# A 16-step gated recurrence in closed form: the scale of A moved into the gates, and 1 + d - t summed on TensorE

## The chip, the cores and the metric

The kernel runs on one core of a Trainium2 chip. The metric is the device time of one execution in microseconds, the median of three runs. The engines named below are TensorE (PE in the profile; its weight loads are PEld), VectorE (DVE), ScalarE (ACT), GpSimd (POOL) and SyncE (SP, which issues most of the transfers). Each engine works through its own queue of instructions in order; semaphores hold an instruction until the ones that it depends on, on other engines, are done.

## The reference

Four layers are applied one after the other to an image of 256 x 256 pixels and 128 channels in float32, each as x = x + layer(groupnorm(x)): an attention along rows, a gated complex recurrence, a triangle product and a convolution with a projection. The change concerns the second, cut here to what matters (c is 64, the channels are 64 real and 64 imaginary ones):

```python
forget_gate = jax.nn.sigmoid(x_ri @ Wf + bf + 2.0)
input_gate = jax.nn.sigmoid(x_ri @ Wi + bi)
delta = jax.nn.softplus(x_ri @ Wd + bd) * 0.1
A_f = _pad_and_fft(A_real, A_imag, h, w, k)
B_f = _pad_and_fft(B_real, B_imag, h, w, k)
...
mag = jnp.sqrt(Ar ** 2 + Ai ** 2 + 1e-08)
scale = 0.95 * jax.nn.sigmoid(mag) / (mag + 1e-08)
Ar = Ar * scale
Ai = Ai * scale
...
inp_r = delta[..., :c] * input_gate[..., :c] * Bx_r
inp_i = delta[..., c:] * input_gate[..., c:] * Bx_i
fg_r, fg_i = (forget_gate[..., :c], forget_gate[..., c:])
def step(h_state, _):
    h_r, h_i = h_state
    Ah_r = Ar * h_r - Ai * h_i
    Ah_i = Ar * h_i + Ai * h_r
    return ((fg_r * Ah_r + inp_r, fg_i * Ah_i + inp_i), None)
h0 = (jnp.zeros_like(x_r), jnp.zeros_like(x_i))
(h_r, h_i), _ = jax.lax.scan(step, h0, None, length=T)      # T = 16
```

For every pixel and channel, a step multiplies the pair (h_r, h_i) by a 2 x 2 matrix M and adds the same input v. M has the trace t = (fg_r + fg_i) Ar and the determinant d = fg_r fg_i (Ar^2 + Ai^2). The kernel doesn't run the 16 steps: it gets their sum from t, d, powers of M by repeated squaring, and a division by D = 1 + d - t.

## The kernel before

The recurrence (function `recurrence`) works on 64 blocks of 4 image rows. A block is held as tiles of 128 partitions (two halves of the block times 64 channels) by 2 x 512 elements (real and imaginary part, 512 pixels each), called wide in the code, or by 512 elements, called thin. All is float32.

A block passes through some seventy steps, each a small function of one or a few instructions of one engine. They are put in order by hand, in the list `order` at the end of the function: each entry is a step and a lag. Iteration `it` runs the list once, each step on block `it` minus its lag, so three blocks are in work at a time. `pin` keeps every engine's instructions in that order. Each engine's queue is therefore the list, filtered for that engine.

For TensorE one iteration is, with the block's lag in brackets: av (2), m2 (0), zb (1), pox, po1, po2 (2), zf (0), zi (1), bx (1), zd (0), za (0), pa (1), and av again. In the profile m2 is shown as m, and the three parts of po as po<-xf, po<-t and po<-yf. zd, zf and zi are the gates' products of weights and x. za and zb are the spectra of A and B. m2 and pa are sums of two squares, by an identity matrix (`ident`) as the weights and accumulation in PSUM; bx and av are complex products, summed in the same way with `ident` and its negative (`negid`). A float32 matmul shows as two passes.

For VectorE the end of an iteration and the beginning of the next are: s, u4, A, tr8, qg, u8, v (reads bx), xa, y1, y0, tr16, ff, xb, d_, pf, be, t, e_, yf (reads av), al, D_, t1, yb, tr2, p0, p1 (they read zb), u2, q, tr4. In the profile xa, xb and be show as g, y0 and y1 as y, t1, e_ and al as t, yb as yf, and p0 and p1 as p.

The steps around the change: za gives the unscaled A; zaa (ScalarE) copies it to `ar`; a2 and m2 give its squared magnitude; lm, mg, lb, iv, sg (ScalarE) and s (VectorE) give the scale s. A multiplies `ar` by s. A2 (ScalarE) squares the result, pa sums the two squares, d_ multiplies pa by ff = fg_r fg_i. pf gives fg_r + fg_i, t multiplies it by the real part of A, D_ makes 1 + d - t, and lD and eD (ScalarE: Ln and Exp) make the division. y0 and y1 multiply v by A, yf multiplies the result by f.

PSUM places are shared by tags: the gates and spectra rotate through two places ("z"), av, bx and po share a single one ("y"), m2 and pa rotate through two ("s"). A tile that takes a place waits until the readers of its predecessor are done. On ScalarE, Ln and Exp on the one hand and the sigmoids on the other need different tables, and the order keeps each group together, with two table loads for an iteration.

Of the kernel before, what the change touches and what calls it, by code (L numbers as in the profile page):

```python
# [10 lines left out]
AF = mybir.ActivationFunctionType  # L11
# [6 lines left out]
P = 128  # L18
N = 256
# [11 lines left out]
class Kernel:  # L31
# [808 lines left out]
    def recurrence(self, x1T, x2T, HD_, stats1, shift1, stats2, shift2):  # L840
# [5 lines left out]
        MUL, ADD, SUB, MAX = ALU.mult, ALU.add, ALU.subtract, ALU.max  # L846
        NB = N // 4
        with ExitStack() as c:
# [3 lines left out]
            negid = wp.tile([P, P], F32, name="negid")  # L852
            V.tensor_scalar_mul(negid, self.ident, -1.0)
            gw, gb = {}, {}
            with self.pool(name="rwp", bufs=2, space=PSUM) as ps0:
                ab, mg, _ = self.group_affine(wp, ps0, stats1, self.g4, "1", True, shift=shift1)
# [22 lines left out]
            D = [{} for _ in range(NB)]  # L879
            rows = lambda t: t.rearrange("p i (r v) -> p r i v", v=N)  # L880
            both = lambda t: t.unsqueeze(1).to_broadcast([P, 2, 512])
# [4 lines left out]
            def act(out, in_, func, **kw):  # L886
                want = tables.get(func)
                if want not in (None, current[0]):
                    pin(nc.scalar.preload_act_table_set(want))  # L889
                    current[0] = want  # L890
                return pin(self.act(out, in_, func, **kw))
# [13 lines left out]
            def wide(d, n, bufs=1):  # L905
                d[n] = tp.tile([P, 2, 512], F32, name=n, tag="w" + n, bufs=bufs)
                return d[n]

            def thin(d, n, bufs=1):
                d[n] = tp.tile([P, 512], F32, name=n, tag="h" + n, bufs=bufs)  # L910
                return d[n]

            def tt(out, a, b_, op):
                pin(V.tensor_tensor(out, a, b_, op))  # L914

            def stt(out, a, k, b_, op0, op1):
                pin(V.scalar_tensor_tensor(out, a, k, b_, op0, op1))  # L917
# [15 lines left out]
            def total(d, name, pairs):  # L933

                n = len(pairs)
                z = d[name] = ps.tile([P, n, 512], F32, name=name, tag="y" if n == 2 else "s", bufs=1 if n == 2 else 2)
                for i, terms in enumerate(pairs):
                    for k, (m, t) in enumerate(terms):
                        pin(self.mm(z[:, i], m, t, start=k == 0, stop=k == len(terms) - 1))

            def real_and_imaginary(d, name, p0, p1):

                total(d, name, [[(self.ident, p0[:, 0]), (negid, p1[:, 1])], [(self.ident, p0[:, 1]), (self.ident, p1[:, 0])]])

            def halves(d, out, name, z, func):
                for ri in range(2):
                    act(out[:, ri], d[z][:, ri], func, bias=gb[name][:, ri:ri + 1])
# [22 lines left out]
            def f(d): halves(d, wide(d, "f", 2), "f", "zf", AF.Sigmoid)  # L970
            def zi(d): gate(d, "i")
            def ig(d): halves(d, wide(d, "ig"), "i", "zi", AF.Sigmoid)
            def zaa(d): act(wide(d, "ar"), d["za"].rearrange("p r i v -> p i r v"), AF.Copy)
            def A(d):
                sb = d["s"].rearrange("p (r v) -> p r v", v=N).unsqueeze(2).to_broadcast([P, 2, 2, N])
                tt(rows(wide(d, "A", 2)), rows(d["ar"]), sb, MUL)
            def A2(d): act(wide(d, "A2"), d["A"], AF.Square)
            def pa(d): total(d, "pa", [[(self.ident, d["A2"][:, 0]), (self.ident, d["A2"][:, 1])]])
            def ff(d): tt(thin(d, "ff"), d["f"][:, 0], d["f"][:, 1], MUL)
            def pf(d): tt(thin(d, "fs"), d["f"][:, 0], d["f"][:, 1], ADD)  # L980
            def t(d): tt(thin(d, "t", 2), d["fs"], d["A"][:, 0], MUL)
            def d_(d): tt(thin(d, "d", 2), d["pa"][:, 0], d["ff"], MUL)
            def D_(d): stt(thin(d, "D", 2), d["d"], 1.0, d["t"], ADD, SUB)

            def xn(d):
                wide(d, "xn")
# [26 lines left out]
            def tr16(d): stt(thin(d, "tr16"), d["dn8"], -2.0, d["tq16"], MUL, ADD)  # L1013
            def xa(d): stt(thin(d, "g", 2), d["t"], -2.0, d["u8"], ADD, MUL)
            def xb(d): tt(d["g"], d["g"], d["tr16"], SUB)
            def lD(d): act(d["D"], d["D"], AF.Ln)
            def eD(d): act(d["D"], d["D"], AF.Exp, bias=math.log(0.5), scale=-1.0)
            def be(d): stt(d["g"], d["g"], 2.0, d["D"], ADD, MUL)
            def e_(d): stt(d["t"], d["t"], -1.0, d["g"], ADD, MUL)
            def al(d): tt(d["t"], d["u8"], d["t"], SUB)  # L1020

            def y0(d): tt(wide(d, "y0"), d["A"], both(d["v"][:, 0]), MUL)
            def y1(d): tt(wide(d, "y1"), d["A"], both(d["v"][:, 1]), MUL)
            def av(d): real_and_imaginary(d, "av", d["y0"], d["y1"])
            def yf(d): tt(wide(d, "yf"), d["av"], d["f"], MUL)
            def t1(d): tt(wide(d, "t1"), both(d["t"]), d["v"], MUL)
# [6 lines left out]
            def ordered(d, t, stop):  # L1033
                for half in range(2):
                    hs = slice(half * HC, (half + 1) * HC)
                    for ri in range(2):
                        pin(self.mm(d["po"][ri * HC:(ri + 1) * HC, half], self.ident[hs, hs], t[hs, ri], start=False, stop=stop))
# [7 lines left out]
            def bn(d):  # L1045
# [4 lines left out]


            order = (
                (zd, 0), (y0, 2), (tr16, 2), (za, 0), (xn, 1), (ff, 1), (A2, 1), (ab, 0), (pa, 1), (av, 2), (ae, 0),
                (xb, 2), (d_, 1), (eD, 2), (pf, 1), (a2, 0), (al_, 0), (be, 2), (zaa, 0), (dn2, 1), (t, 1), (dn4, 1),
                (m2, 0), (e_, 2), (lm, 0), (yf, 2), (zb, 1), (al, 2), (D_, 1), (t1, 2), (yb, 2), (pox, 2), (tq2, 1),
                (po1, 2), (po2, 2), (mg, 0), (tr2, 1), (lb, 0), (lD, 1), (zf, 0), (p0, 1), (p1, 1), (iv, 0), (u2, 1),
                (sg, 0), (tq4, 1), (ev_, 2), (f, 0), (q, 0), (tr4, 1), (s, 0), (dn8, 1), (zi, 1), (u4, 1), (A, 0),
                (bx, 1), (tq8, 1), (ig, 1), (tr8, 1), (qg, 1), (bn, 2), (u8, 1), (tq16, 1), (v, 1), (xa, 1), (y1, 1),
            )
            deep = max(lag for _, lag in order)  # L1060
# [525 lines left out]
```

## Time and profile before

| | |
|---|---|
| median of 3 runs | 5087.27 us (5086.96 to 5087.37) |
| span of the profiled execution, first to last instruction | 5083.0 us |
| its granted TensorE clock | 0.995 of full |
| attention and the first norm | up to about 1700 us |
| recurrence | about 1700 to 3219 us |
| triangle product and convolution | from about 3219 us |
| busy over the whole span | PE 4951.9, DVE 4100.4, ACT 3496.8, POOL 406.9 us |

The median stands 4.3 us above the span of the profiled execution. The shares over the whole span are averages over stages with different limits; the recurrence has to be read by itself. A matmul in the timeline is given its start and a modelled length; consecutive ones overlap, so the distance from start to start is the better measure of what one takes. "x4" in such a line is four passes, and the bracket at the end gives the idle time of the engine just before and what ended it.

### The profile page before, as it was taken

The numbers are of one execution on the slowest core, as the hardware profiler recorded it, in microseconds if no ns is written. First come the engines' busy times: TensorE is split into PE (matmuls) and PEld (weight loads), VectorE is DVE, ScalarE is ACT, GpSimd is POOL, SyncE is SP. The second block draws the span as 40 slices with busy tenths as digits, with TensorE's granted clock in tenths as the row PEclk, the third lists the DMA queues.
The fourth block names the chain that finished last, engine by engine and source line by source line (L and its number), as shares of the span: only waits on it lengthen the run. The fifth ranks groups of instructions, "written<-read, shape, count | busy, mean of one in ns | idle before, by whom it ended". The sixth has DMA issues, their size and how long they took to land.

```text
span 5083.0 us, 78992 instructions
## 1 busy us (share of the span) xinstructions
PE 4951.9 (97%) x31563; PEld 2715.8 (53%) x31563; DVE 4100.4 (81%) x4797; ACT 3496.8 (69%) x4948; POOL 406.9 (8%) x592
## 2 busy tenths in 40 slices
PE   8999999999999899999999999899999999999999
PEld 2444555555555333333333333329999953359999
DVE  6666999999999799999999999775333537779886
ACT  6445888888888899999999999453333357762110
POOL 0331000000000000000000000240111010000000
PEclk9999999999999999999999999999999999999999
DMA  8894222222222222222222221688667778865432
GB/s 290 292 338 173 88 80 84 84 80 88 84 80 84 68 68 68 72 64 76 64 73 67 72 68 60 218 324 309 237 229 243 252 286 321 324 233 180 142 122 67
DMA packets 204463, 781.69 MB, mean 154 GB/s; under 512 B 56278, under 2 KB 59628, under 8 KB 154788
## 3 DMA queue, kind: packets, MB, share of 16 engines
q1 hardware_dynamic: 146638, 505.57, 29.8%
q0 software_dynamic: 56160, 270.64, 14.8%
q8 instruction: 252, 4.13, 0.3%
q14 instruction: 117, 0.96, 0.1%
q10 hardware_dynamic: 1296, 0.40, 0.0%
HBM read 505.18 MB, written 271.32 MB: 153 GB/s over the span
## 4 chain that ended last, share of the span: by engine, by line
PE 57%; DVE 29%; issue 5%; ACT 1%; POOL 0%; DMA 0%; POOLq 0%; DVEq 0%; SPq 0%; ACTq 0%
PE z L60 9%; PE m L60 7%; PE nd L60 7%; PE sc L60 5%; PE zc L60 5%; PE po L60 4%; DVE tr L917 3%; DVE t L914 3%; DVE y L914 3%; DVE p L914 3%; DVE yf L914 3%; PE ppq L60 3%; PE ppv L60 2%; PE px L60 2%; PE pe L60 2%
## 5 line engine op out<-in xcount | busy, mean ns | idle before, releaser
L576 DVE TENSOR_TENSOR e<-sc,bT 128x1024 f32<-128x1024 f32 x512 | 603.1, 1220 | 49.8 <-PE sc L60 48.9
L54 ACT ACTIVATE e<-e 128x1024 f32<-128x1024 f32 x512 | 540.4, 1055 | 61.5 <-DVE e L576 52.4
L1077 DVE TENSOR_TENSOR LR<-z,sg 128x512 f32<-128x512 f32 x256 | 268.4, 1049 | 363.0 <-ACT sg L54 363.0
L60 PE MATMUL m<-U,v 128*128 128x128 f32 x4608 | 514.8, 275 | 0.0
L60 PEld LDWEIGHTS m<-U,v 128*128 128x128 f32 x4608 | 514.6, 192 | 0.0
L60 PE MATMUL z<-wf,zt 128*128 128x128 f32 x4096 | 459.6, 276 | 1.4 <-DVE zn L1077 1.4
L60 PEld LDWEIGHTS z<-wf,zt 128*128 128x128 f32 x4096 | 459.4, 192 | 2.3 <-DVE zn L1077 2.2
L54 ACT ACTIVATE sg<-z 128x512 f32<-128x512 f32 x256 | 152.9, 597 | 307.7 <-PE z L60 307.7
L54 ACT ACTIVATE sq<-zs 128x1024 f32<-128x1024 f32 x192 | 202.4, 1054 | 192.1 <-DVE zs L385 156.1
L576 DVE TENSOR_TENSOR ks<-e 128x1024 f32<-128x1024 f32 x256 | 301.0, 1217 | 0.0
L60 PE MATMUL sc<-tq,tk 32*128 32x256 f32 x4096 | 297.0, 401 | 3.0 <-DVE e L576 2.1
L60 PEld LDWEIGHTS sc<-tq,tk 32*128 32x128 f32 x4096 | 186.4, 184 | 159.6 <-issue 96.3
L60 PE MATMUL nd<-e,tv 128*32 128x256 f32 x4096 | 271.0, 382 | 0.0
L54 ACT ACTIVATE dn<-dn 128x512 f32<-128x512 f32 x384 | 241.9, 630 | 13.0 <-DVE dn L576 2.3
L60 PE MATMUL av<-y,ident 128*128 128x512 f32 x384 | 192.9, 611 | 44.0 <-DVE y L914 44.0
L60 PE MATMUL po<-LR 128*128 128x256 f32 x1024 | 222.2, 380 | 6.9 <-DVE LR L1077 6.9
L1462 ACT COPY m4s<-m 128x512 f32<-128x512 f32 x32 | 18.7, 583 | 287.2 <-PE m L60 287.2
L60 PEld LDWEIGHTS po<-LR 128*128 128x128 f32 x1024 | 194.1, 190 | 34.2 <-DVE LR L1077 7.7
L60 PE MATMUL bx<-p,ident 128*128 128x512 f32 x384 | 192.4, 610 | 0.0
L54 ACT ACTIVATE o<-po 128x256 f32<-128x256 f32 x256 | 84.3, 381 | 145.3 <-issue 110.5
L60 PEld LDWEIGHTS nd<-e,tv 128*32 128x32 f32 x4096 | 120.1, 109 | 108.2 <-issue 42.1
L889 ACT ACT_TABLE_LOAD x132 | 169.4, 1283 | 1.5
(366 smaller groups left out, 10321.1 us busy)
## 6 DMA issues: line engine op xcount, KB each, us to landing
zt<-znT SPq DMA_DIRECT2D x128, 1024.0 KB
znT<-zn POOLq DMA_DIRECT2D x64, 1024.0 KB, 5.2
xin<-x2T SPq DMA_DIRECT2D x64, 1024.0 KB
xin<-in_x_dram SPq DMA_DIRECT2D x50, 1024.0 KB
xr<-x3T SPq DMA_DIRECT2D x46, 768.0 KB
xT<-xo POOLq DMA_DIRECT2D x32, 1024.0 KB, 9.3
xr<-xT SPq DMA_DIRECT2D x64, 512.0 KB
zn<-znT SPq DMA_DIRECT2D x64, 512.0 KB
```

Of the source, the lines that this page charges most:

```text
L54: return self.nc.scalar.activation(out, in_, func, bias=bias, scale=scale, **kw)
L60: return self.nc.tensor.matmul(out, lhsT, rhs, start=start, stop=stop)
L576: pin = lambda f: lambda *a, **k: tc.keep_in_program_order(f(*a, **k))
L889: pin(nc.scalar.preload_act_table_set(want))
L914: pin(V.tensor_tensor(out, a, b_, op))
L917: pin(V.scalar_tensor_tensor(out, a, k, b_, op0, op1))
L1077: pin = lambda f: lambda *a, **k: tc.keep_in_program_order(f(*a, **k))
L1462: nc.scalar.copy(m4, m[4])
```

## The change

The scale s is no longer multiplied into A. It is multiplied into both forget gates instead, in place (`fs_`), which gives the same M, since every entry of M is a product of a gate and a part of A. A is then used unscaled as `ar` (now with two buffers, for it lives on until y0). The determinant is the product of the scaled gates times the unscaled squared magnitude, which m2 holds already; so the square A2 and its sum pa go. 1 + d - t is no longer made by VectorE: TensorE sums d and minus t in PSUM as pD (a tile of tag "s"), and lD reads that and adds the 1 as the bias of its Ln. In the list, D_ keeps its place, fs_ takes that of A, and A2 and pa leave.

```diff
-            def zaa(d): act(wide(d, "ar"), d["za"].rearrange("p r i v -> p i r v"), AF.Copy)
-            def A(d):
-                sb = d["s"].rearrange("p (r v) -> p r v", v=N).unsqueeze(2).to_broadcast([P, 2, 2, N])
-                tt(rows(wide(d, "A", 2)), rows(d["ar"]), sb, MUL)
-            def A2(d): act(wide(d, "A2"), d["A"], AF.Square)
-            def pa(d): total(d, "pa", [[(self.ident, d["A2"][:, 0]), (self.ident, d["A2"][:, 1])]])
+            def zaa(d): act(wide(d, "ar", 2), d["za"].rearrange("p r i v -> p i r v"), AF.Copy)
+            def fs_(d): tt(d["f"], d["f"], both(d["s"]), MUL)
             def ff(d): tt(thin(d, "ff"), d["f"][:, 0], d["f"][:, 1], MUL)
             def pf(d): tt(thin(d, "fs"), d["f"][:, 0], d["f"][:, 1], ADD)
-            def t(d): tt(thin(d, "t", 2), d["fs"], d["A"][:, 0], MUL)
-            def d_(d): tt(thin(d, "d", 2), d["pa"][:, 0], d["ff"], MUL)
-            def D_(d): stt(thin(d, "D", 2), d["d"], 1.0, d["t"], ADD, SUB)
+            def t(d): tt(thin(d, "t", 2), d["fs"], d["ar"][:, 0], MUL)
+            def d_(d): tt(thin(d, "d", 2), d["m2"][:, 0], d["ff"], MUL)
+            def D_(d): total(d, "pD", [[(self.ident, d["d"]), (negid, d["t"])]])
...
-            def lD(d): act(d["D"], d["D"], AF.Ln)
+            def lD(d): act(thin(d, "D", 2), d["pD"][:, 0], AF.Ln, bias=1.0)
...
-            def y0(d): tt(wide(d, "y0"), d["A"], both(d["v"][:, 0]), MUL)
-            def y1(d): tt(wide(d, "y1"), d["A"], both(d["v"][:, 1]), MUL)
+            def y0(d): tt(wide(d, "y0"), d["ar"], both(d["v"][:, 0]), MUL)
+            def y1(d): tt(wide(d, "y1"), d["ar"], both(d["v"][:, 1]), MUL)
...
-                (zd, 0), (y0, 2), (tr16, 2), (za, 0), (xn, 1), (ff, 1), (A2, 1), (ab, 0), (pa, 1), (av, 2), (ae, 0),
+                (zd, 0), (y0, 2), (tr16, 2), (za, 0), (xn, 1), (ff, 1), (ab, 0), (av, 2), (ae, 0),
...
-                (sg, 0), (tq4, 1), (ev_, 2), (f, 0), (q, 0), (tr4, 1), (s, 0), (dn8, 1), (zi, 1), (u4, 1), (A, 0),
+                (sg, 0), (tq4, 1), (ev_, 2), (f, 0), (q, 0), (tr4, 1), (s, 0), (dn8, 1), (zi, 1), (u4, 1), (fs_, 0),
```

The helper `total` makes pa, m2 and pD; it takes a PSUM tile of tag "s" for a single sum:

```python
z = d[name] = ps.tile([P, n, 512], F32, name=name, tag="y" if n == 2 else "s", bufs=1 if n == 2 else 2)
for i, terms in enumerate(pairs):
    for k, (m, t) in enumerate(terms):
        pin(self.mm(z[:, i], m, t, start=k == 0, stop=k == len(terms) - 1))
```

## The prediction

> **What bounds the kernel now.** I read the page first: TensorE (PE) is busy 97% of the span and VectorE (DVE) 81%, which does not say what limits the stage that the change touches. So next the busy time in stretches, for 600 us inside the recurrence:
>
> ```profile
> core 0: us, PE busy (x) PEld busy (x) DVE busy (x) ACT busy (x) POOL busy (x), PEclk, DMA share, GB/s
> 1900.00:2500.00 600.00, 583.98 (x1959) 194.21 (x1958) 600.00 (x749) 578.08 (x850) 13.88 (x26) 1.00 0.22 69
> ```
>
> VectorE has no gap at all: it is the bound. PE is short of it by 16 us in 600, ScalarE (ACT) by 22. But a PE busy time also counts matmuls stretched by waits, so the third view is the timeline of one steady iteration, PE first, then VectorE (start us, length us, engine, line, operation, tiles, idle before):
>
> ```profile
> 2204.48 1.10 PE L60 MATMUL av<-y,ident 128*128 128x512 f32 x2 [0.61 <-DVE y L914]
> ...
> 2207.99 1.88 PE L60 MATMUL m<-a,ident 128*128 128x512 f32 x4
> ...
> 2218.64 1.13 PE L60 MATMUL bx<-p,ident 128*128 128x512 f32 x2
> 2219.60 1.02 PE L60 MATMUL bx<-p,negid 128*128 128x512 f32 x2
> 2220.46 1.88 PE L60 MATMUL bx<-p,ident 128*128 128x512 f32 x4
> 2222.27 1.94 PE L60 MATMUL zd<-xf,gwd 128*64 128x512 f32 x8
> 2224.14 1.13 PE L60 MATMUL za<-ev,hs 14*128 14x512 f32 x4
> 2225.19 1.98 PE L60 MATMUL pa<-A,ident 128*128 128x512 f32 x4
> 2227.79 1.10 PE L60 MATMUL av<-y,ident 128*128 128x512 f32 x2 [0.61 <-DVE y L914]
> ...
> 2223.55 1.22 DVE L917 SCALAR_TENSOR_TENSOR v<-q,bx 128x1024 f32<-128x1024 f32 x1
> 2224.68 0.69 DVE L917 SCALAR_TENSOR_TENSOR g<-t,u 128x512 f32<-128x512 f32 x1
> 2225.28 2.36 DVE L914 TENSOR_TENSOR y<-A,v 128x1024 f32<-128x1024 f32 x2
> 2227.56 0.69 DVE L917 SCALAR_TENSOR_TENSOR tr<-dn,tq 128x512 f32<-128x512 f32 x1
> ```
>
> Two things are to be seen. The period is 23.30 us (av starts at 1738.75 in the first such iteration and 3160.06 in the last: 1421.31 / 61 = 23.30). And there is a loop round two engines: av on PE, then PE's queue down to bx, then v on VectorE (it reads bx), xa (shown as g), y1 and y0 (shown as y), and av of the next iteration. bx ends at 2220.46 + 1.88 = 2222.34, v starts at 2223.55: the loop has slack there, VectorE comes to v late because it is full. How long the loop is without that slack, the first full iteration shows, in which PE was late and VectorE waited:
>
> ```profile
> 1732.19 1.88 PE L60 MATMUL bx<-p,ident 128*128 128x512 f32 x4
> 1734.11 1.22 DVE L917 SCALAR_TENSOR_TENSOR v<-q,bx 128x1024 f32<-128x1024 f32 x1 [0.32 <-PE bx L60]
> 1738.75 1.02 PE L60 MATMUL av<-y,ident 128*128 128x512 f32 x2
> ...
> 1742.18 1.88 PE L60 MATMUL m<-a,ident 128*128 128x512 f32 x4
> 1743.99 1.13 PE L60 MATMUL zb<-ev,hs 14*128 14x512 f32 x4
> 1745.05 1.98 PE L60 MATMUL po<-xf,ident 128*128 128x512 f32 x4
> 1746.96 1.09 PE L60 MATMUL po<-t,ident 64*64 64x512 f32 x8
> 1747.87 1.04 PE L60 MATMUL po<-yf,ident 64*64 64x512 f32 x8
> 1748.84 1.94 PE L60 MATMUL zf<-xf,gwf 128*64 128x512 f32 x8
> 1750.64 1.94 PE L60 MATMUL zi<-xf,gwi 128*64 128x512 f32 x8
> 1752.51 1.12 PE L60 MATMUL bx<-p,ident 128*128 128x512 f32 x2
> ```
>
> v starts 0.04 us after bx ends (1732.19 + 1.88 = 1734.07), so a closed loop costs that. PE from av to bx took 1752.51 - 1738.75 = 13.76 us here, against 14.16 (2218.64 - 2204.48) in the steady state, where PE is held back a little at po and zi by VectorE. [...]
>
> [...] in both iterations above the matmuls come in the same order, and an early one never passes a late one. So the place of the new sum in PE's queue matters, not only its size. [...] the trace has 0.69, but successive ones start 0.60 apart, and 0.60 is what a removed one gives back. [...] Here pa is slow (3.25 us in place of 1.98) already behind a gap of 2.63 us at 3180.55, while 4 passes behind one of 1.32 us at 3213.86 took the usual 1.98; below I check the gap that arises.
>
> **The change, part by part**, for one iteration.
>
> VectorE: the product A (1024 wide) becomes f times s (1024 wide, one operand repeated over the two halves as in y0 and y1, 1.22 us): nothing either way. d_ reads m2 in place of pa, both in PSUM: nothing. D_ goes: -0.60 us. Its removal puts t1 directly behind al, whose result it reads; where an instruction follows its own source (fs then t, 1719.58 to 1720.30) starts are 0.72 apart, so +0.12. VectorE's work: 23.30 - 0.60 + 0.12 = 22.82 us. If that were all: 61 x -0.48 = -29 us.
>
> ScalarE: A2 goes, 0.95 us from start to start (2223.89 to 2224.83). lD reads PSUM: lm does that in 0.60 where lD takes 0.61 to 0.63; nothing. ScalarE is not the bound, so nothing is gained beyond room: lD now waits for the end of pD instead of D_. By the sums below pD ends 8.3 us after av, and lD starts in the steady iteration at 2212.11 - 2204.48 = 7.63, so iv, the table load, sg and the rest behind it move by about 0.7 us. f then ends at about 14.5 after av, and the product f times s comes up on VectorE at 15.0; qg, which needs ig, is ready near 16.8 against 16.7. Both stay 0.7 us short of where bx will let v go.
>
> TensorE: pa goes (4 passes, between za and av) and pD comes (4 passes, between zb and po). The total is equal, the place is not. pa stood behind bx, where PE waits for y0 in any case: its removal only lengthens the idle time before av. pD stands between av and bx, in the loop. Its price: bx is the same pattern as pD and po together, ident, negid, ident: 2222.27 - 2218.64 = 3.63 us. po alone takes 1746.96 - 1745.05 = 1.91. So pD adds 1.72 us. It doesn't wait itself: d and t are ready 2.3 and 4.1 us after av, pD starts at 6.4. Behind it in PE's queue stand po, zf, zi and bx; all move by 1.72 and bx takes v with it. Their own waits (yf, t1, yb, p1) are then long done. m2 is kept until d_ of the next iteration, at 1.6 to 2.3 us after av; the next m2 starts at 3.5 in the other place, and of the two PSUM buffers of that tag pa's goes to pD: nothing.
>
> The loop after the change: 13.76 (av to bx without holding) + 0.08 (av behind an idle PE, 2207.99 - 2204.48 = 3.51 against 3.43) - 0.03 (zf, held by p1 in that iteration; in the stage's first iteration zf takes 1706.97 to 1708.74 = 1.77) + 1.72 = 15.53 to the start of bx; + 3.70 to its end (2218.64 to 2222.34); + 0.04 to v; + 4.24 from v to av (2223.55 to 2227.79, VectorE's fixed order). Sum 23.51 us. Without pD it is 21.79, so the loop had 1.51 us of slack and the change puts 1.72 in it. VectorE at 22.82 is then no longer the bound and idles 0.7 us before v. PE's own work, 23.51 less 4.28 for the way from bx over v to av, plus zd and za beside it (1.87 + 1.05), is 22.15: it idles 1.4 us before av. That is about the gap of 1.32 us that did no harm, so I charge nothing for the clock.
>
> 61 periods x (23.51 - 23.30) = +12.8 us. Beginning and end: the first d no longer waits for A2 and pa (the trace has VectorE idle 4.8 us there, but most of it lies on other chains), worth -1 to -2; at the end pa leaves and pD comes in the chain: +1 to +2. Taken as 0, plus or minus 2. Span 5083.0 + 12.8 = 5095.8; the median of the runs stands 4.3 above the span, so 5100 us.
>
> Unknown costs, both ends: pD 1.60 (if ident behind zb comes as cheap as elsewhere) to 1.85 us; v after bx 0.0 to 0.1; av after the longer gap 0 to 0.1. A period of 23.35 to 23.75, +3 to +27 us: 5090 to 5114.
>
> **Rivals.** (a) The loop is shorter than I make it, VectorE stays the bound and the saved D_ counts: 22.82, 5087 - 29 = 5058 us. For it: VectorE at 600 of 600. Against: it needs pD to cost under 1.03 us on PE, or PE's 13.76 to hold 0.7 us of waiting that I took for work. The sign turns at a pD of 1.51 us. (b) Between the two: loop and old period agree within 0.1 us, 5081 to 5093, if more than I think of PE's time at po, zf and zi is waiting. (c) The moved ScalarE chain: if f and ig come over 1 us later than worked out, f times s holds VectorE's queue, and v waits for qg, not bx; a period of 24.1, +49, 5136 us. For it: ScalarE 578 of 600 busy. Against: A2's 0.95 us is gone. A clock that drops in the 1.4 us gap would be worse still.
>
> **How the numbers follow.** Main case 0.60, (a) 0.10, (b) 0.17, (c) with the clock 0.13. What can be told from no change is 0.2%, 10 us: 5077 to 5097. About three quarters of the main case lies above. Faster 0.11, same 0.28, slower 0.61. The range leaves out (a) and half of (c): 5083 to 5122; the main case's own is 5090 to 5114.
>
> **What would show it.** Right: v with an idle time before it released by PE bx in every iteration; av's idle at about 1.4 us; av to av 23.5; pD to po 1.8 us. Wrong: VectorE again full with a period under 23; or v's wait released by ScalarE.

## The result, and the profile after

| | before | changed |
|---|---|---|
| median | 5087.11 us | 5121.19 us |
| lowest to highest of 4 runs | 5086.85 to 5087.37 | 5118.82 to 5127.68 |
| ratio, 95% interval | 1 | 1.0069 (1.0055 to 1.0084) |
| span of the profiled execution | 5083.0 us | 5119.4 us |
| its mean TensorE clock | 0.995 | 0.99 |

The change makes the kernel slower by 0.7%, 34 us, where +13 was predicted. The stretch of the recurrence that was shown of before reads after the change (busy time of each engine, then granted clock, DMA share and GB/s):

```profile
core 0: us, PE busy (x) PEld busy (x) DVE busy (x) ACT busy (x) POOL busy (x), PEclk, DMA share, GB/s
1900.00:2500.00 600.00, 566.20 (x1906) 198.24 (x1904) 578.22 (x703) 539.69 (x805) 13.31 (x25) 0.98 0.24 68
```

No engine is full any more: VectorE idles 22 us in 600, TensorE 34. The two queues wait for each other. And the clock, 1.00 before, is 0.98. The timeline of a usual iteration, TensorE and then VectorE:

```profile
2218.14 1.10 PE L60 MATMUL av<-y,ident 128*128 128x512 f32 x2 [1.35 <-DVE y L914]
...
2224.52 1.13 PE L60 MATMUL pD<-d,ident 128*128 128x512 f32 x2
2225.48 1.02 PE L60 MATMUL pD<-t,negid 128*128 128x512 f32 x2
2226.34 1.88 PE L60 MATMUL po<-xf,ident 128*128 128x512 f32 x4
...
2233.61 1.13 PE L60 MATMUL bx<-p,ident 128*128 128x512 f32 x2
...
2235.43 1.88 PE L60 MATMUL bx<-p,ident 128*128 128x512 f32 x4
...
2241.59 1.10 PE L60 MATMUL av<-y,ident 128*128 128x512 f32 x2 [1.35 <-DVE y L914]
...
2235.51 1.22 DVE L914 TENSOR_TENSOR q<-q,ig 128x1024 f32<-128x1024 f32 x1 [0.37 <-ACT ig L54]
2236.65 0.68 DVE L914 TENSOR_TENSOR u<-u,tr 128x512 f32<-128x512 f32 x1
2237.35 1.22 DVE L917 SCALAR_TENSOR_TENSOR v<-q,bx 128x1024 f32<-128x1024 f32 x1
```

v starts at 2237.35, 0.04 us after the end of bx (2235.43 + 1.88 = 2237.31): the loop is closed, as forecast, though with little to spare: u starts at 2236.65 and v could follow it at 2237.25, so the way over ScalarE (f, ig, then q) is only 0.10 us shorter than the one over bx. The period is 2241.59 - 2218.14 = 23.45 us. That alone gives 61 x (23.45 - 23.30) = +9 us. But from the first av to the 62nd it is 1458.69 us (1739.16 to 3197.85), 37.4 more than before. The rest lies in 17 of these 61 iterations, which last 25.1 us, 1.67 longer (one of them is the first, which starts behind a gap of 2.55 us). One of them, and the clock in it:

```profile
1808.72 1.13 PE L60 MATMUL za<-ev,hs 14*128 14x512 f32 x4
1811.20 2.05 PE L60 MATMUL av<-y,ident 128*128 128x512 f32 x2 [1.35 <-DVE y L914]
1813.04 1.79 PE L60 MATMUL av<-y,negid 128*128 128x512 f32 x2
1814.67 1.88 PE L60 MATMUL av<-y,ident 128*128 128x512 f32 x4
```

```profile
1811.20:1814.60 3.40, 3.40 (x4) 1.48 (x5) 3.40 (x7) 3.38 (x4) 0.00 (x0) 0.50 0.13 34
1814.60:1818.00 3.40, 3.40 (x9) 1.33 (x7) 2.68 (x5) 2.45 (x4) 0.00 (x0) 1.00 0.00 0
```

The first two passes of av take 1.84 us from start to start in place of 0.94, and the granted clock is 0.50 for the 3.40 us from the start of av on and 1.00 right after. So 17 x 1.67 = 28 us are a TensorE at half clock behind its gap, and 28 + 9 = 37. The other 44 iterations have the same za and the same gap, and the clock stays whole; why is seen when the clock is read in steps of 3.41 us, first round the gap of the slow iteration, then round that of the usual one above:

```profile
1807.75:1811.16 3.41, 2.10 (x10) 0.44 (x6) 3.41 (x5) 2.67 (x4) 0.00 (x0) 1.00 0.43 118
1811.16:1814.57 3.41, 3.37 (x4) 1.52 (x5) 3.41 (x6) 3.38 (x5) 0.00 (x0) 0.50 0.14 36
2213.93:2217.35 3.42, 2.86 (x12) 0.65 (x11) 3.42 (x4) 2.68 (x5) 0.00 (x0) 1.00 0.19 53
2217.35:2220.76 3.41, 2.62 (x6) 1.25 (x7) 3.41 (x6) 3.38 (x4) 0.00 (x0) 1.00 0.37 105
```

All 26 drops in this profile begin within 0.01 us of one grid of steps of 3.413 us, and all but the last, at the end of the execution, end on it. In the slow iteration za (1.13 us) and nearly the whole gap fall into a single step, which leaves about 1.0 us of matmuls of 128 rows in it (2.10 less za); the next step runs at half clock. In the usual one the border of two steps, 2217.35, cuts the gap in two, and there are 1.7 and 2.6 us of them in the two steps.

### The profile page after: what moved, and what is told of

It reads as the page before. It is cut to its first block, busy times and chain, and to the rows that moved or that the text cites. A ratio compares the mean times of both kernels' runs of the same rounds, so it can differ in the third digit from the quotient of the medians.

```text
span 5119.4 us, 78864 instructions
## 1 busy us (share of the span) xinstructions
PE 4939.4 (96%) x31563; PEld 2735.1 (53%) x31563; DVE 4083.2 (80%) x4733; ACT 3434.6 (67%) x4884; POOL 405.6 (8%) x592
## 4 chain that ended last, share of the span: by engine, by line
PE 73%; DVE 9%; ACT 5%; issue 3%; DMA 0%; POOL 0%; POOLq 0%; DVEq 0%; ACTq 0%; SPq 0%
PE m L60 9%; PE po L60 9%; PE z L60 9%; PE nd L60 7%; PE sc L60 5%; PE av L60 5%; PE zc L60 5%; DVE y L914 3%; PE ppq L60 3%; PE ppv L60 2%; PE px L60 2%; PE pD L60 2%; PE zf L60 2%; PE pe L60 2%; PE ppg L60 2%
## 5 line engine op out<-in xcount | busy, mean ns | idle before, releaser
L60 PE MATMUL av<-y,ident 128*128 128x512 f32 x384 | 208.2, 653 | 94.8 <-DVE y L914 94.8
L60 PEld LDWEIGHTS av<-y,ident 128*128 128x128 f32 x384 | 73.9, 207 | 217.0 <-issue 217.0
```

Source lines behind the costliest of these rows:

```text
L60: return self.nc.tensor.matmul(out, lhsT, rhs, start=start, stop=stop)
```

## The experiments

All are compared with the kernel before on the same chip, whose median was 5085.6 to 5086.4 us there; versions from different chips are best compared by their ratios. My theory was that the gap before av lets the clock drop; the rivals were that something else does it, and that the cost is in the new sum as such.

| | median, us | ratio to before (95%) | usual period, us | iterations of over 24.6 us, of 61 |
|---|---|---|---|---|
| changed kernel | 5121.19 | 1.0069 (1.0055 to 1.0084) | 23.45 | 17 |
| e1 gap filled, 128 rows | 5092.53 | 1.0013 (1.0006 to 1.0019) | 23.38 | 1 |
| e2 gap filled, 14 rows | 5127.41 | 1.0081 (1.0064 to 1.0098) | 23.38 | 19 |
| e3 scale in the gates alone | 5122.12 | 1.0071 (1.0054 to 1.0088) | 23.89 | 0 |
| e4 sum moved before av | 5057.19 | 0.9941 (0.9924 to 0.9957) | 22.83 | 0 |
| e5 e3 with filled gap | 5083.65 | 0.9996 (0.9987 to 1.0004) | 23.31 | 0 |
| e6 sum in PSUM alone | 5114.35 | 1.0055 (1.0039 to 1.0070) | 23.77 | 0 |
| e7 half of e1's fill | 5092.34 | 1.0010 (1.0004 to 1.0017) | 23.38 | 1 |
| e8 e4 and yb before t1 | 5045.34 | 0.9919 (0.9905 to 0.9932) | 22.70 | 0 |
| e9 za before zd | 5135.67 | 1.0095 (1.0078 to 1.0112) | 24.00 | 1 |

The period is from av to av in the profiled execution; for the kernel before it is 23.31 us by the same measure, with none over 24.6. The single long one of e1, e7 and e9 is the first, which starts behind the slow beginning of the stage; the first is also among the 17 and the 19. e3 has none over 24.6 because every one of its iterations is slow.

**e1, the gap filled.** The edit to the changed kernel, of which e2 takes 14 rows (`ident[0:14]`, `xf[0:14, 0:512]`) and e7 256 columns:

```diff
-            def av(d): real_and_imaginary(d, "av", d["y0"], d["y1"])
+            def av(d):
+                z = d["av"] = ps.tile([P, 2, 512], F32, name="av", tag="y", bufs=1)
+                pin(self.mm(z[:, 0], self.ident, d["xf"][:, 0:512]))
...
```

The lines left out are av's own two sums, written out.

> The changed kernel plus one matmul (two passes of 128 rows by 512 columns, about 0.96 us) that lies in the 1.35 us gap of TensorE before av; it writes the place that av overwrites, so nothing waits for it and the path over bx, v, y1, y0 stays as it is. Theory 'clock': the gap is what drops TensorE's clock in every third or fourth iteration; with the gap down to about 0.4 us no iteration starts at half clock, all periods are 23.45 us, and the time falls by some 17 x 1.68 = 28 us to 5090 to 5095. Rival 'something else slows every third iteration' (a transfer, ScalarE's tables, the load of the new sum): still 17 slow iterations of 25.1 us and 5118 to 5124; more work on TensorE can then only cost.

It came as the clock theory has it: 5092.53. The gap in TensorE's timeline is 0.20 us, and the clock 1.00 (third column from the end):

```profile
2207.57 1.13 PE L60 MATMUL za<-ev,hs 14*128 14x512 f32 x4
2208.62 1.12 PE L60 MATMUL av<-xf,ident 128*128 128x512 f32 x2
2209.95 1.12 PE L60 MATMUL av<-y,ident 128*128 128x512 f32 x2 [0.20 <-DVE y L914]
```

```profile
1900.00:2500.00 600.00, 594.68 (x1992) 206.14 (x1991) 589.66 (x720) 551.72 (x821) 13.35 (x25) 1.00 0.24 69
```

A matmul whose result is thrown away makes the kernel 0.56% faster (1.0069 to 1.0013). What is left, 0.13%, is the closed loop and the slow first iteration.

**e2, the same with 14 rows.**

> The same fill, but of 14 rows in place of 128: TensorE is occupied for the same time by a matmul that uses a ninth of the array's rows. Theory 'idle time': only idle time counts for the clock, so as with the fill of 128 rows all periods are 23.45 us and the time is 5090 to 5095. Rival 'activity by rows': a matmul of few rows counts little, as za (14 rows too) does just before the gap; then slow iterations stay, and the time is 5105 to 5121.

The idle time falls to 0.41 us, and the clock drops all the same (0.98 from 1900 to 2500 us), in 19 iterations. The timeline of one of them:

```profile
2238.92 1.13 PE L60 MATMUL za<-ev,hs 14*128 14x512 f32 x4
2239.88 1.02 PE L60 MATMUL av<-xf,ident 14*128 14x512 f32 x2
2241.30 2.02 PE L60 MATMUL av<-y,ident 128*128 128x512 f32 x2 [0.41 <-DVE y L914]
```

So it isn't idle time alone that counts here. With the matmul of 14 rows in the gap 19 iterations were long, with one of 128 rows a single one, the first (e1, and e7 below with more idle time, 0.63 us, than the 0.41 here). My range for that rival, 5105 to 5121, was too low: I had thought that 14 rows would help a little.

**e3, the scale in the gates alone.** The edit to the changed kernel:

```diff
-            def D_(d): total(d, "pD", [[(self.ident, d["d"]), (negid, d["t"])]])
+            def D_(d): stt(thin(d, "D", 2), d["d"], 1.0, d["t"], ADD, SUB)
...
-            def lD(d): act(thin(d, "D", 2), d["pD"][:, 0], AF.Ln, bias=1.0)
+            def lD(d): act(d["D"], d["D"], AF.Ln)
```

> The first half of the change alone: the scale in the gates, A2 and pa gone, but 1 + d - t made by VectorE as before, so nothing new stands between av and bx. VectorE's work is what it was, 23.30 us a period; TensorE has 1.9 us less to do and idles about 2.5 us before av. Theory 'clock': the longer gap drops the clock in more iterations than the 17 of the changed kernel; each costs av some 1.7 us, of which the loop's slack of 1.5 us takes nearly all, so the time is 5085 to 5100 with TensorE's mean clock lower than 0.98 in the stage. Rival 'the new sum is what drops the clock': clock 1.00 and 5083 to 5088.

The new sum isn't there, and the clock drops in every iteration (0.93 from 1900 to 2500 us), which rules out the rival. But 5122.12 is outside my range: I had set the slow av against the slack of the way over v, and it is read earlier, by yf. TensorE and VectorE:

```profile
2216.57 2.04 PE L60 MATMUL av<-y,ident 128*128 128x512 f32 x2 [2.06 <-DVE y L914]
2218.40 1.57 PE L60 MATMUL av<-y,negid 128*128 128x512 f32 x2
...
2221.73 1.23 DVE L914 TENSOR_TENSOR yf<-av,f 128x1024 f32<-128x1024 f32 x1 [0.50 <-PE av L60]
```

yf finds VectorE waiting 0.50 us; it starts 0.58 us later than it would straight behind its neighbours, which follow each other at 0.60. VectorE has as much work as before and no slack, so the 0.58 us goes into every period (23.89 against 23.31). This kernel does strictly less work than the one before, A2 and pa having gone, and takes some 36 us longer.

**e5, e3 with the gap filled** by two matmuls of 128 rows and 512 columns (four passes, as pa had):

> The first half of the change alone (as in e3), plus two matmuls of 128 rows by 512 columns (four passes, 1.8 us) before av, in the place where pa stood; their result is overwritten by av. In e3 every iteration had its clock halved at av, and yf, which reads av on the full VectorE, came 0.5 us late. Theory 'clock': it was the lack of work that cost the time; with the meaningless matmuls the gap is about 0.6 us, the clock 1.00, VectorE full again with 23.30 us, and the time 5083 to 5090. Rival 'the scale in the gates costs by itself' (its place on VectorE, the wait for f): 5115 to 5125 as in e3.

The time is that of before within the interval, 0.9996 (0.9987 to 1.0004). The scale in the gates costs nothing by itself; VectorE is full again, 600 of 600 us, and the clock 1.00. That pa goes cost e3 some 36 us at a clock of 0.93; with the fill in its place the clock is 1.00 and the loss gone.

**e7, a shorter fill.**

> The changed kernel with half of e1's fill: one matmul of 128 rows by 256 columns before av (about 0.5 us), which leaves a gap of about 0.85 us behind it. Theory 'stretch without full-row work': za (14 rows, 1.05 us) and the gap count together; a stretch of 2.4 us drops the clock in 17 of 61 iterations, one of 3.1 (e3) in all, one of 1.3 (e1) in none; a fill between za and the gap cuts the stretch in two, so few or no slow iterations: 5090 to 5098. Rival 'sum of the window': what counts is the work in a window of 3.4 us, not an unbroken stretch, and a few slow iterations stay: 5098 to 5112.

A fill of half the length does as well as the whole, though 0.63 us of idle time stay behind it:

```profile
2206.43 1.13 PE L60 MATMUL za<-ev,hs 14*128 14x512 f32 x4
2207.48 0.70 PE L60 MATMUL av<-xf,ident 128*128 128x256 f32 x2
2208.81 1.12 PE L60 MATMUL av<-y,ident 128*128 128x512 f32 x2 [0.63 <-DVE y L914]
```

The window of 3.4 us in its rival is the length of a drop in the changed kernel (3.41 us). The run does not tell the two theories apart, for no step of 3.41 us has less than 1.79 us of matmuls of more than 14 rows here. The trace of the changed kernel does: behind equal stretches, 2.4 us, the clock drops in 16 of 60 iterations and not in the others, and the two kinds differ by the work in the step (last section).

**e9, the same gap behind other work.** In the list, za and zd change places:

```diff
-                (zd, 0), (y0, 2), (tr16, 2), (za, 0), (xn, 1), (ff, 1), (ab, 0), (av, 2), (ae, 0),
+                (za, 0), (y0, 2), (tr16, 2), (zd, 0), (xn, 1), (ff, 1), (ab, 0), (av, 2), (ae, 0),
```

> The changed kernel with za (14 rows) put in front of zd (128 rows) in TensorE's queue: the same work and the same gap of about 1.35 us before av, but the gap now follows full-row work and no longer za. ScalarE gets zd 1.05 us later, so ab, ae and eD come up to 1 us later, still ahead of be. Theory 'za and the gap count together': the stretch without full-row work is 1.35 us, as in e1, and no iteration starts at half clock: period 23.45, 5088 to 5097. Rival 'the gap alone, or the work in a window of 3.4 us whatever its order': za still lies in the same window, slow iterations of 25.1 us stay, 5110 to 5124. Rival 'ScalarE is late': a period over 23.6 us with full clock, 5097 to 5110.

None of the three came whole. For the clock the first is right: the gap before av is still 1.35 us, directly behind zd's 128 rows now, and the clock is 1.00 with no drop behind it. But the time is worse, for the reason of the third rival in a size that I had not worked out. The timeline of TensorE and of VectorE:

```profile
2198.39 1.94 PE L60 MATMUL zd<-xf,gwd 128*64 128x512 f32 x8
2201.68 1.10 PE L60 MATMUL av<-y,ident 128*128 128x512 f32 x2 [1.35 <-DVE y L914]
...
2205.64 1.99 PE L60 MATMUL m<-a,ident 128*128 128x512 f32 x4 [0.28 <-ACT a L54]
...
2204.71 0.69 DVE L917 SCALAR_TENSOR_TENSOR g<-g,D 128x512 f32<-128x512 f32 x1 [0.17 <-ACT D L54]
```

```profile
1900.00:2500.00 600.00, 559.02 (x1901) 191.14 (x1900) 578.59 (x701) 534.02 (x801) 13.32 (x25) 1.00 0.23 67
```

zd comes 1.05 us later to ScalarE, with it ab, ae, the table load, eD and a2, and m2, which stands in TensorE's queue inside the loop, waits for a2. m2 starts 3.96 us after av in place of 3.51 and takes 0.10 longer to zb; these 0.55 us are the whole way from 23.45 to 24.00 us a period. With that period every iteration lies 0.11 us later on a grid of 3.41 us than the one before, so that the 61 pass over a whole step, and no place in it brought a drop after the first iteration. So here the clock was whole and the loss, 0.55 us a period, came by way of ScalarE's queue.

**e6, the sum in PSUM alone.** The kernel before with D_ and lD as in the changed kernel (the reverse of e3's edit):

> The second half alone: the kernel before, with A, A2 and pa, but 1 + d - t made by TensorE behind zb. pa fills the gap before av, so the clock holds; but then TensorE's own work is the longest: 15.45 to the start of bx, 3.63, zd 1.87, za 1.05, pa 1.82, in all 23.8 us a period with no gap, against 23.43 for the loop over v. Theory: +0.5 x 61 = +31 us, 5112 to 5124, with clock 1.00 and no gap before av. Rival 'the loop over v alone': 23.45 a period, 5095. Rival 'VectorE': 22.82, 5057.

5114.35, a period of 23.77 with full clock and no gap: pa (1.82 us) follows za and av follows pa without a pause.

```profile
1900.00:2500.00 600.00, 600.00 (x2017) 214.26 (x2014) 582.12 (x709) 563.49 (x833) 13.35 (x25) 1.00 0.24 68
```

So with pD added and pa left in place TensorE's own work is the bound. The changed kernel has less TensorE work than this and is no faster.

**e4, the sum moved.** D_ goes to where pa stood, one iteration later, and lD with it:

```diff
-                (zd, 0), (y0, 2), (tr16, 2), (za, 0), (xn, 1), (ff, 1), (ab, 0), (av, 2), (ae, 0),
-                (xb, 2), (d_, 1), (eD, 2), (pf, 1), (a2, 0), (al_, 0), (be, 2), (zaa, 0), (dn2, 1), (t, 1), (dn4, 1),
+                (zd, 0), (y0, 2), (tr16, 2), (za, 0), (xn, 1), (ff, 1), (ab, 0), (D_, 2), (av, 2), (ae, 0),
+                (xb, 2), (d_, 1), (lD, 2), (eD, 2), (pf, 1), (a2, 0), (al_, 0), (be, 2), (zaa, 0), (dn2, 1), (t, 1), (dn4, 1),
...
-                (m2, 0), (e_, 2), (lm, 0), (yf, 2), (zb, 1), (al, 2), (D_, 1), (t1, 2), (yb, 2), (pox, 2), (tq2, 1),
-                (po1, 2), (po2, 2), (mg, 0), (tr2, 1), (lb, 0), (lD, 1), (zf, 0), (p0, 1), (p1, 1), (iv, 0), (u2, 1),
+                (m2, 0), (e_, 2), (lm, 0), (yf, 2), (zb, 1), (al, 2), (t1, 2), (yb, 2), (pox, 2), (tq2, 1),
+                (po1, 2), (po2, 2), (mg, 0), (tr2, 1), (lb, 0), (zf, 0), (p0, 1), (p1, 1), (iv, 0), (u2, 1),
```

> The changed kernel with the new sum moved in the list from behind zb to the place that pa had, between za and av, one iteration later, and lD with it to just before eD. Theory 'place': the loop av, bx, v, y0, av is then 21.8 us, VectorE is the bound with 22.82 us (no gap), TensorE idles about 0.6 us before av and keeps its clock: 5087 - 0.48 x 61 = 5058, 5052 to 5065. Rival 'amount': if the cost of the change were in the sum as such (PSUM traffic, ScalarE's wait for it), it stays above 5087; ScalarE, which now waits for pD just before eD, could also hold be on VectorE and give 5065 to 5090.

5057.19, with the same operations as the changed kernel, 64 us apart by place alone. TensorE, then VectorE:

```profile
2216.10 1.13 PE L60 MATMUL za<-ev,hs 14*128 14x512 f32 x4
2217.16 1.12 PE L60 MATMUL pD<-d,ident 128*128 128x512 f32 x2
2218.12 1.02 PE L60 MATMUL pD<-t,negid 128*128 128x512 f32 x2
2219.69 1.10 PE L60 MATMUL av<-y,ident 128*128 128x512 f32 x2 [0.54 <-DVE y L914]
...
2202.56 0.70 DVE L914 TENSOR_TENSOR t<-u,t 128x512 f32<-128x512 f32 x1
2203.29 1.23 DVE L914 TENSOR_TENSOR t<-t,v 128x1024 f32<-128x1024 f32 x1
```

pD, work of 128 rows, lies in the gap, out of the loop, and the clock is 1.00 (1900 to 2500 us). VectorE is the bound again with 22.83 us a period (599 of 600 us busy), and the D_ that it lost now counts. What can still be won is the place of t1, 0.73 us behind al, whose result it reads.

**e8, e4 with yb between the two** (and po's two parts exchanged in TensorE's queue, with their accumulation flags):

```diff
-            def po1(d): ordered(d, d["t1"], False)
-            def po2(d): ordered(d, d["yf"], True)
+            def po1(d): ordered(d, d["t1"], True)
+            def po2(d): ordered(d, d["yf"], False)
...
-                (m2, 0), (e_, 2), (lm, 0), (yf, 2), (zb, 1), (al, 2), (t1, 2), (yb, 2), (pox, 2), (tq2, 1),
-                (po1, 2), (po2, 2), (mg, 0), (tr2, 1), (lb, 0), (zf, 0), (p0, 1), (p1, 1), (iv, 0), (u2, 1),
+                (m2, 0), (e_, 2), (lm, 0), (yf, 2), (zb, 1), (al, 2), (yb, 2), (t1, 2), (pox, 2), (tq2, 1),
+                (po2, 2), (po1, 2), (mg, 0), (tr2, 1), (lb, 0), (zf, 0), (p0, 1), (p1, 1), (iv, 0), (u2, 1),
```

> The version of e4 (sum before av), with yb put between al and t1 on VectorE, and the two parts of po in TensorE's queue exchanged to match. In e4 t1 follows al, whose result it reads, 0.73 us after it in place of 0.60; with yb between them that 0.13 us goes. Theory 'VectorE is the bound': 22.83 - 0.13 = 22.70 us a period, 61 x -0.13 = -8 us against e4: 5046 to 5052. Rival: TensorE, with 0.4 us left before av, or ScalarE takes over: 5054 to 5060.

22.70 us a period, the 0.13 us of the expectation, and 5045.34 us in all: 0.9919 (0.9905 to 0.9932) of the kernel before, the fastest of the versions. That is just under the range of 5046 to 5052: the 61 periods account for 8 of the 12 us, as expected, and in the two profiles another 3 us lie ahead of the first av, where nothing of the edit has run yet. VectorE is full and the clock 1.00:

```profile
1900.00:2500.00 600.00, 589.27 (x2021) 202.47 (x2019) 600.00 (x740) 572.84 (x848) 14.37 (x27) 1.00 0.22 70
```

## Why the prediction was right or wrong

- The direction and its cause were right: pD stands in the loop av, bx, v, y0, av, and the loop takes VectorE's place as the bound. The time lies just inside the upper end of the range, 5122, and above that of the main case, 5114. That the range holds it is luck: it was drawn so wide for half of the case of a late ScalarE, and what filled it was the clock.
- The sum of the loop was right, and with it the step from TensorE's order to its time: in the profiles the matmuls come in the order of the list in each iteration that lies whole between 1739 and 3160 us, 60 before and 59 after. Predicted 15.53 us to the start of bx, measured 15.47 (2218.14 to 2233.61); 3.70 for bx, measured the same; 0.04 to v and 4.24 from v to av, both the same. Period 23.51 predicted, 23.45 measured: +9 us in place of +12.8.
- VectorE's 22.82 us without D_, an instruction of 512 elements (0.69 us long, 0.60 from its start to the next, 2210.80 to 2211.40 before), was right. e4 shows it as 22.83, the +0.12 behind al included; so was the gain of 29 us that stays hidden behind the loop (e4: 28 us between the medians).
- The gap before av was right, 1.35 us against 1.4.
- ScalarE's shift was right in kind and too small: q (qg) comes 17.37 us after av in place of 16.8, having waited 0.37 us for ig, and v could then start only 0.10 us before bx lets it go, not 0.7. So the sign that was named for a right prediction, an idle time before v, did not appear: the 0.37 us lie ahead of q. It costs nothing, but by a narrow margin.
- The step that failed is the price of the gap before av: "That is about the gap of 1.32 us that did no harm, so I charge nothing for the clock." It measured 17 iterations of 1.67 us, 28 us, three quarters of the whole loss. Two things were wrong in it. One harmless case, 1.32 us, was taken for a rule, with a single case of harm, 2.63 us, beside it; in the changed kernel itself 44 of the 61 gaps did no harm, so that one says little. And the gap was looked at without what stands before it: the 1.32 us lay behind av, 128 rows, the 1.35 us lie behind za, 14 rows. e1, e2, e7 and e9 show that this counts: 1, 19, 1 and 1 long iterations. The rival that could have carried the price got one sentence without a number.
- The case (a), VectorE's gain, was not what happened, but e4 and e8 show that only the place of the sum kept it away.

## What to carry to other kernels

When two engines wait for each other round an iteration, add up the loop with each queue's own order, and put new work where that queue waits anyway; with the sum in one place this change cost 0.7%, with it in another it brought 0.6%. Before taking work off TensorE, look at what fills its gaps: here a fill of 128 rows without use brought the clock from 0.98 to 1.00 and the time down by 29 us (e1), and one of 14 rows brought neither (e2, 0.98 and 6 us more). When a slow iteration returns every third or fourth time, read the granted clock in windows of a few microseconds (0.50 over 3.40 us here) instead of the mean, which hides it (0.98).

## What the runs showed of the hardware that was not expected

- The clock dropped behind a stretch with no matmul of 128 rows of 2.4 us (za 1.06 and a gap of 1.35) in 16 of the 60 iterations after the first, behind one of 3.1 us (e3: za 1.06 and 2.06) in all of them, behind one of 1.35 us (e9) in none. In e7 two stretches of about 1.06 and 0.63 us with half a microsecond of 128 rows between them did no harm. A number of rows between 14 and 128 was not tried in a fill.
- The drops keep to a grid. In the profiles of the kernel before and of the changed one every drop (12 and 26 of them) begins within 0.01 us of a grid of steps of 3.413 us, one grid for the whole of each execution; in the recurrence of the changed kernel the starts of neighbouring drops, from the first iteration to the 61st, lie 71.68 or 95.57 us apart, 21 or 28 steps. In e3 the slow av returns after 23.89 us, 7 steps.
- What went before a drop is a step with little work of more than 14 rows. Summed from the modelled lengths of the matmuls in the traces, without those of 14 rows, the step ahead of a drop has at most 1.19 us of 3.41 in the changed kernel, and every other step of its 61 iterations at least 1.24; in e2 1.10 and 1.15, after the first iteration; in e3 0.77 and 2.43. In e1, e7 and e9 no step after the first iteration up to the 62nd av has less than 1.79 us, and there is no drop. So in these traces the steps ahead of a drop differ from the others by their work, and an equal stretch brings a drop in one place on the grid and none in another. From these sums I estimate the border at about 1.2 us, and no closer than a few tenths: e2 has a step of 1.15 us without a drop, the changed kernel one of 1.19 with a drop, and in the first iterations of e1 and e2 drops stand behind 1.49 and 1.28 us.
- The drops tie the iteration to the grid. A usual iteration of 23.45 us is 0.44 short of seven steps, 23.89, and moves the gap back on the grid; a slow one, 1.67 longer, moves it forward again. To stay in place, 60 iterations need 60 x 0.44 / 1.67 = 16 slow ones, and 16 were measured; for e2, 60 x 0.51 / 1.70 = 18, and 18 were measured. e3 has each one slow, at 23.89. So three kernels with different work take the same time for 61 periods, 1458.69, 1458.65 and 1457.57 us, and what e3 saves in the loop is lost to the clock. The sums fit; no run shifted the grid.
